# A four-layer graph network on one core: moved feature loads, wider-spaced row tiles, dense rows in two steps, and one last store

## The chip, the cores and the metric

The kernel runs on one core of one Trainium2 chip. The metric is the device time of one execution in microseconds (us). Beside it stands a profile of one execution: a page, and a trace that can be asked for waits, stretches and single instructions. The engines are called PE (matrix multiplication), DVE (VectorE), ACT (ScalarE), POOL (GpSimd) and SP (SyncE). DVE, ACT and POOL compute; SP only issues transfers here, and ACT and POOL issue some too.

## The reference

There are 2708 nodes with 512 features each, and one sparse matrix `adj`, stored densely. Four layers follow each other, each as `x = layernorm(x + layer(x))`, all in float32:

- Layer 0: `adj` plus its mask, scaled by row, times `x`, over the row's sum.
- Layer 1: attention and graph convolution, joined by two gates: `sigmoid(gate_a * (attn @ (x @ W_sa)) + gate_b * (adj @ (x @ W_gcn) + b))`, where the attention weights come from `exp(-leaky_relu(s_left + s_right))` on the entries of `adj` that are not zero.
- Layer 2: `x @ W0 + A x @ W1 + A A x @ W2 + A A A x @ W3`, so three products with `adj` in a row.
- Layer 3: `relu((D (adj + I) D @ x + x) @ W + b)`, with `D` from the degrees.

So nearly all of the work is seven products of a 2708 x 2708 matrix with a 2708 x 512 one.

## The kernel before, in words

**Tiling.** Rows of `adj` are cut into two halves of 1354, features into two halves of 256, so that every product is a 2 x 2 block product. It is done with seven block products instead of eight (the scheme of Strassen and Winograd): DVE first makes sums of the blocks of the moving matrix (`s1` to `s4`) and of the features (`T1` to `T4` from `B11`, `B12`, `B21`, `B22`, functions `x_sums` and `x_last`), PE then runs the seven products P1 to P7 into the PSUM banks `accu`, `accc`, `accd` and `acca`, and DVE adds the products to the result. Of the 1354 rows, ten tiles have 128 rows; the 74 rows that remain of each half are handled apart ("R" groups, loaded by `rest_x`, bank `accr`).

**Stages.** The seven products are stages S[0] to S[6]. Stages 0 to 2 are run by `sweep` over the four column ranges `RANGES` (0, 384, 768 and 1024, the last one 330 wide), stages 3 to 6 by `sweep2` over two column ranges `RANGES2` of 338 and 339 with more of the recursion. In the trace stage 0 begins at about 20 us, stage 1 at 429, stage 2 at 830, stage 3 at 1440, and stages 4, 5 and 6 at 1803, 2164 and 2525.

**Order.** `at(position, fn)` puts a piece of work on a list with a position; a stage is 28 positions long, and the list is sorted by position. Each piece then issues its instructions on the engines that it names, and a scheduler fixes the order of each engine from this list; for the first pieces of the kernel and for those marked `hold` (the last argument of `at`) the order of the list is binding. A position thus moves an instruction in its engine's queue, and sets no time. A load is queued on the engine that issues it, and if the load has to wait, everything behind it on that engine waits as well.

**What the change touches.**

- `next_x` (L252) loads the features of the next `sweep` stage. Row tiles 0 to 7 are loaded early; tiles 8 and 9 (group D) and the remainder rows come last, since their source rows were just written. All go on GpSimd's queue, through `x_load` and `rest_x`. The row tile itself (o, X) is normalised by `layernorm` (L552 to L566), whose power (L559) is a GpSimd instruction too, and written to X by GpSimd (`store`, L151).
- `next_x2` (L302) does the same for the `sweep2` stages; `rest` (in it) loads the remainder rows.
- `move` (L147) cuts a transfer in two, so that the first has a multiple of 16 rows:

```
c = m - m % 16 if m > 16 else m
queue.dma_start(out=dst[:c], in_=src[:c])
if c < m:
    queue.dma_start(out=dst[c:m], in_=src[c:m])
```

- `done1` (L994) finishes a column range of stage 1. For the first three ranges it takes pairs of row tiles (one of each half, 3, 3 and 2 of them), and makes the dense product of a pair by `seven` (L637), in two parts, each with matmuls (L644) and sums on DVE (L651). Around them stands the work of the next column range: its products (L457), sums of blocks (`comb`, L402), copies (L511) and sums (`add`, L518) of the products, and the degree tally `deg` (L963), which reads each adjacency tile as it arrives.
- `ext_sums` (L1169) makes four sums (L1180) of dense rows for the later stages: it loads four tiles of X2T (L1176, SP's queue) into tiles of a ring of 38, adds, and stores the sums as Es (L1181, GpSimd's queue). Around it stand the block sums of `sweep2` (z, L1218; t, L1252), the sums of the products (q, L1295; with `accr`, L1353), and the transposes and stores of Y (L1397, L1402).
- `done6` finishes stage 6: a dense product (`ps_d`, L605), two DVE operations (L1479, L1480), the normalisation with its last step on ACT (L564), and the store to `out`. The last row tile has 83 rows.

Of the kernel before, what the change touches and what calls it, by code (L numbers as in the profile page):

```python
# [27 lines left out]
NH = 1354  # L28
# [13 lines left out]
RANGES2 = [(0, 338), (676, 339)]  # L42
# [26 lines left out]
def gnn_kernel(ctx: ExitStack, tc: tile.TileContext, x, adjT, w_sa, a_sa, w_gcn, b_gcn, wab, bab, w_hop, w_out,  # L69
# [108 lines left out]
    def at(pos, fn, hold=False):  # L178

        def go():  # L180
            n = len(nc.cur_bb.bb.instructions)
            fn()
            held.update(range(n, len(nc.cur_bb.bb.instructions)))

        events.append((pos, len(events), go if hold else fn))
# [60 lines left out]
    def x_load(src, k, s, eng):  # L246
        w = wt(k)
        q = x_source(src, k)[("B11", "B12", "B21", "B22").index(s)]
        t = b12_tile(k) if s == "B12" else new_x(s, k)
        move(eng, t[:w], q)  # L250

    def next_x(base, src, sums=0.95, halves=-0.25):  # L252


        q = nc.gpsimd
        at(base + 1.3, lambda: rest_x(src, q))
        for k in range(KW):
            f = k / KT
            if (k * P) < RANGES[-1][0]:
                at(base - 5.8 + f, lambda k=k: x_load(src, k, "B11", q))  # L260
                at(base - 1.85 + f, lambda k=k: x_load(src, k, "B22", q))
                at(base - 1.84 + f, lambda k=k: x_load(src, k, "B12", q))
                at(base - 1.15 + f, lambda k=k: x_sums(k), True)
                at(base - 0.85 + f, lambda k=k: x_load(src, k, "B21", q))
                at(base + 1.5 + f, lambda k=k: x_last(k), True)
            else:
                at(base + halves + 0.05 * (k - 8), lambda k=k: x_load(src, k, "B22", q))
                at(base + max(halves, 0.1) + 0.05 * (k - 8), lambda k=k: x_load(src, k, "B21", q))
                at(base + sums + 0.03 * (k - 8), lambda k=k: x_sums(k), True)
                at(base + 2.6 + 0.03 * (k - 8), lambda k=k: x_last(k), True)  # L270

# [30 lines left out]
    def next_x2(base, src, ext_src=None, one=False, plus=False, swapped=False):  # L302

        q = nc.gpsimd
        m = RANGES2[1][0] // P
        early = {"B11": (-5.8, m), "B12": (-4.8, m)}
        if one:
            early["B22"] = (-0.95, RANGES[-1][0] // P)

        def go(s, ks, ext):  # L310
            for k in ks:
                x_load(src, k, s, q)
            if ext and ext_src is not None:
                c0 = HD if s in ("B12", "B22") else 0
                for i, g in enumerate("BD"):
                    r0 = (HD if s in ("B21", "B22") else 0) + i * P
                    h = "T3" if s == "B12" else s
                    if g == "D" and ks[-1] < 8:
                        group(h, g)
                    t, w = groups[h, g][0][:, 2, :], ext_src[r0 : r0 + P, :]  # L320
                    if not swapped:
                        nc.scalar.dma_start(out=t, in_=w[:, c0 : c0 + HD])
                        continue
                    for f in range(2):
                        nc.scalar.dma_start(out=t[:, f * P : (f + 1) * P].rearrange("p (c d) -> p c d", d=32),
                                            in_=w.rearrange("p (c f d) -> p f c d", c=4, d=32)[:, c0 // P + f, :, :])

        def residual(s):

            for i, g in enumerate("BD"):  # L330
                t = groups[s, g][0][:, 2, i * P : (i + 1) * P]
                nc.vector.tensor_tensor(t, t, ident, ALU.add)

        if plus:
            at(base - 1.4, lambda: residual("B22"), True)
            at(base + 1.9, lambda: residual("B11"), True)
        for s, p in (("B22", 0.0 if one else -1.95), ("B21", 0.02), ("B11", 1.6), ("B12", 1.8)):
            ks = list(range(KW))
            if s in early:
                lo, m = early[s]  # L340
                at(base + lo, lambda s=s, m=m: go(s, range(m), True))
                ks = range(m, KW)
            at(base + p, lambda s=s, ks=ks: go(s, ks, ks[0] == 0))

        def sums(g):
            i = slice(0, 2 if g in "BD" and ext_src is None else 3)
            part = lambda t: t[:, i, :]
            for s in ("T1", "T2", "T4"):
                group(s, g)
            t = {s: part(groups[s, g][0]) for s in SETS}  # L350
            nc.vector.tensor_tensor(t["T1"], t["T3"], t["B11"], ALU.subtract)
            nc.vector.tensor_tensor(t["T2"], t["B22"], t["T1"], ALU.subtract)
            nc.vector.tensor_tensor(t["T3"], t["B22"], t["T3"], ALU.subtract)
            nc.vector.tensor_tensor(t["T4"], t["B21"], t["T2"], ALU.subtract)
            for s in ("T1", "T2", "T3", "T4"):
                groups[s, g][1].update(range(3))

        def rest():
            for e in range(2):
                cols = slice(e * HD, (e + 1) * HD)  # L360
                for s in REST_HOMES[e]:
                    group(s, "R")
                t, t32 = (groups[s, "R"][0] for s in REST_HOMES[e])
                lo, hi = src[KT - 1], src[2 * KT - 1]
                rows_over(q, t, (lo[:, cols], hi[:, cols]))
                q.dma_start(out=t32, in_=copies(hi[KA - KR :, cols], 4))

        at(base + 1.75, rest)
        for i, g in enumerate("ACBD"):
            at(base + 4.2 + 0.3 * i, lambda g=g: sums(g), True)  # L370

# [566 lines left out]
    i = 0  # L938
# [55 lines left out]
    def done1(p0, dp, last, R0, n, h, C, tiles):  # L994
# [39 lines left out]
        for i, (t, lo, w) in enumerate(tiles):  # L1034
            H, y = {}, []

            def b7(part, t=t, lo=lo, w=w, H=H, y=y):
                if part == 0:
                    y.extend(nat("y") for _ in range(2))
                seven(part, Y, W[8], H, lo, w, y, None, [vec[1], vec[1]])  # L1040
                if part == 1:
                    for j in range(2):
                        finish(t + KT * (1 - j), w, y[j])

            at(p0 + 0.6 + 0.56 * i, lambda f=b7: f(0))
            at(p0 + 0.6 + 0.56 * i + 0.26, lambda f=b7: f(1))

    sweep(S[1], RANGES, extra=extra1, done=done1, late=0.85, save=True)

# [116 lines left out]
            move(nc.gpsimd, o[b : b + m, :], src[t][a : a + m, :])  # L1166
        return o

    def ext_sums(g, s, q):  # L1169

        n = RANGES2[g][1]
        E = {}
        for ij in ("11", "21", "22", "12"):
            E[ij] = ring_tile("a" + ij)
            e = (int(ij[1]) - 1) * HD + q * P
            nc.sync.dma_start(out=E[ij][:, :n], in_=X2T[g, int(ij[0]) - 1][e : e + P, s * n : (s + 1) * n])  # L1176
        E["s3"] = ring_tile("s3")
        for m, o, a, b, op in (("s3", "s3", "11", "21", ALU.subtract), ("s1", "21", "21", "22", ALU.add),
                               ("s2", "11", "21", "11", ALU.subtract), ("s4", "12", "12", "11", ALU.subtract)):
            nc.vector.tensor_tensor(E[o][:, :n], E[a][:, :n], E[b][:, :n], op)  # L1180
            nc.gpsimd.dma_start(out=SE[m, g, s][q * P : (q + 1) * P, :], in_=E[o][:, :n])  # L1181

# [197 lines left out]


    for i in range(4):
        at(S[2] + 19.5 + 1.1 * i, lambda i=i: ext_sums(0, i // 2, i % 2))
        at(S[3] + 7.0 + 1.3 * i, lambda i=i: ext_sums(1, i // 2, i % 2))

    def hop_done(dst):

# [77 lines left out]
    def done6(p0, dp, g, i0, n, h, cc, tiles):  # L1465

        end = (g, h) == (1, 0)
        for i, (s, lo, w) in enumerate(tiles[3:] + tiles[:3] if end else tiles):
            got = {}
            r0 = i0 + s * n + lo  # L1470

            def a(r0=r0, w=w, got=got):
                got["x"] = fetch2(X3, h, r0, w)

            def b(s=s, lo=lo, w=w, r0=r0, got=got):
                px = dense(lambda c: cc(s, c)[:, lo : lo + w], W[6], w)
                y = got["x"]
                r = 12 * g + 6 * h + 3 * s + lo // P
                nc.vector.scalar_tensor_tensor(px[:w], px[:w], rdeg_f[:w, r : r + 1], vec[6][:w], ALU.mult, ALU.add)  # L1479
                nc.vector.scalar_tensor_tensor(y[:w], px[:w], 0.0, y[:w], ALU.max, ALU.add)  # L1480
                layernorm([(y, 0, D)], y, w, True)
                move(nc.sync, out[h * NH + r0 : h * NH + r0 + w, :], y[:w])

            p = p0 - 0.095 + 0.14 * i if end else p0 + 0.1 + 0.28 * i
            at(p - 0.6, a)
            at(p, b)
# [57 lines left out]
```

## Time and profile before

| | |
|---|---|
| Median of 7 runs | 2900.22 us (2897.40 to 2902.28) |
| The profiled execution's own time | 2898.14 us |
| Its span, first to last instruction | 2896.3 us |
| Mean granted clock of PE | 0.996 |
| Busy, PE | 2843.6 us |
| Busy, DVE | 2242.1 us |
| Busy, POOL | 626.6 us |
| Busy, ACT | 564.9 us |

Times in the trace are counted from the first instruction. A line of the list of waits reads: engine, tile and line that waited, "<-", the engine (or transfer), tile and line that it waited for, then us in total, how often, and the longest. In a line of a timeline stand the start, the duration, the engine, the line, the operation with what it writes and reads, and in brackets how long the engine had stood idle and what ended that. A PE that is busy may still run at half its clock; the stretches list the granted clock beside the busy time.

### The profile page before, as it was taken

Reading aid. Unit: us, or ns where it says so; the run is one execution under the profiler, and the core shown is the slowest. Engines: PE = TensorE matmul, PEld = TensorE weight load, DVE = VectorE, ACT = ScalarE, POOL = GpSimd, SP = SyncE. Lnnn points to the kernel's source line nnn. Section 1 sums busy time; section 2 is a strip of 40 time slices with the busy share of each in tenths; the row PEclk is TensorE's granted clock in tenths of the full one; section 3 lists DMA queues with packets and bytes.
Section 4 is the critical chain, followed back from the end, with each engine's and each line's share of the span. In section 5 each row is a group of like instructions: output and inputs, shape, how many; then the busy total and the mean of one; then the engine's idle time right before and its main releaser. Section 6 shows DMA issues by size and latency. Waiting matters only on the chain. (4 is left out here: it accounts for less than half of the span.)

```text
span 2896.3 us, 37361 instructions
## 1 busy us (share of the span) xinstructions
PE 2843.6 (98%) x10847; PEld 1852.1 (64%) x10847; DVE 2242.1 (77%) x5780; ACT 564.9 (20%) x1106; POOL 626.6 (22%) x1133
## 2 busy tenths in 40 slices
PE   7999999999999999999999999999999999999998
PEld 6655665658765656766666666666666666665664
DVE  6989698667648675875689788887888878798776
ACT  4544200101137454651100000000000100100001
POOL 0223224123310101123113033030330212501102
PEclk9999999999999999999999999999999999999999
DMA  7666466355544333564667667566675665854551
GB/s 232 202 199 188 137 212 218 110 166 168 179 128 131 116 115 100 176 192 151 207 208 222 205 197 234 168 207 203 200 235 164 197 187 171 240 170 142 174 154 59
DMA packets 373145, 511.50 MB, mean 177 GB/s; under 512 B 64022, under 2 KB 326096, under 8 KB 372940
## 3 DMA queue, kind: packets, MB, share of 16 engines
q1 hardware_dynamic: 307128, 372.01, 43.5%
q0 software_dynamic: 50272, 127.29, 12.9%
q10 hardware_dynamic: 15540, 9.82, 1.2%
q8 instruction: 86, 1.41, 0.2%
q14 instruction: 119, 0.97, 0.1%
HBM read 425.22 MB, written 83.67 MB: 176 GB/s over the span
## 5 line engine op out<-in xcount | busy, mean ns | idle before, releaser
L1218 DVE TENSOR_TENSOR z<-z 128x339 f32<-128x339 f32 (+1 forms) x966 | 456.9, 506 | 12.0 <-PE accu L1271 3.3
L1289 ACT COPY q<-accu 128x338 f32<-128x338 f32 (+1 forms) x84 | 34.5, 443 | 1025.4 <-PE accu L1271 1025.4
L559 POOL TENSOR_TENSOR rstd<-rstd,neg_half 128x1 f32<-128x1 f32 (+3 forms) x92 | 59.2, 643 | 719.1 <-DVE rstd L558 713.4
L1271 PE MATMUL accc<-s,t 128*128 128x338 f32 (+1 forms) x644 | 198.3, 452 | 0.0
L1271 PE MATMUL accu<-z,t 128*128 128x338 f32 (+1 forms) x644 | 194.4, 448 | 0.6 <-DVE z L1218 0.6
L1271 PE MATMUL accc<-z,t 128*128 128x338 f32 (+1 forms) x644 | 193.7, 448 | 0.0
L1271 PE MATMUL accd<-z,t 128*128 128x338 f32 (+1 forms) x644 | 193.7, 448 | 0.0
L1402 POOL DMA_DIRECT2D Y<-y x192 | 104.8, 552 | 378.2 <-DVE y L1397 343.2
L402 DVE TENSOR_TENSOR a<-a,a 128x384 f32<-128x384 f32 (+2 forms) x330 | 162.9, 515 | 10.3 <-PE accu L457 8.9
L1271 PEld LDWEIGHTS accc<-s,t 128*128 128x128 f32 x644 | 121.5, 191 | 65.8 <-issue 8.9
L1271 PEld LDWEIGHTS accd<-z,t 128*128 128x128 f32 x644 | 122.3, 190 | 61.4 <-issue 1.8
L1271 PEld LDWEIGHTS accc<-z,t 128*128 128x128 f32 x644 | 122.1, 190 | 61.6 <-issue 2.4
L1271 PEld LDWEIGHTS accu<-z,t 128*128 128x128 f32 x644 | 121.7, 190 | 61.8 <-issue 1.9
L1218 DVE TENSOR_TENSOR s<-z 128x338 f32<-128x338 f32 (+1 forms) x322 | 150.3, 505 | 8.4 <-PE accc L1271 7.6
L1295 DVE TENSOR_TENSOR q<-q,accd 128x338 f32<-128x338 f32 (+1 forms) x112 | 56.4, 504 | 128.0 <-PE accd L1271 128.0
L1072 ACT ACTIVATE e<-row,neg_s 128x384 f32<-128x384 f32 (+5 forms) x176 | 100.4, 570 | 79.6 <-DVE e L1074 27.5
L1074 DVE TENSOR_TENSOR e<-e,f 128x384 f32<-128x384 f32 (+5 forms) x176 | 87.9, 509 | 22.6 <-ACT f L1073 21.5
L1073 ACT ACTIVATE f<-row,neg_s 128x384 f32<-128x384 f32 (+5 forms) x176 | 100.0, 568 | 27.0 <-PE accc L457 7.1
L963 DVE SCALAR_TENSOR_TENSOR deg<-a,deg 128x384 f32<-128x384 f32 (+2 forms) x152 | 75.2, 506 | 14.5 <-DMA a<-in_adjT 13.5
L605 PE MATMUL ps_d<-w,q 128*128 128x512 f32 (+2 forms) x192 | 85.7, 593 | 0.0
L1075 DVE SCALAR_TENSOR_TENSOR a<-a,e 128x384 f32<-128x384 f32 (+2 forms) x160 | 80.5, 510 | 3.5 <-DMA a<-in_adjT 1.2
L405 POOL DMA_DIRECT2D As<-a x120 | 64.9, 544 | 78.2 <-DVE a L402 68.4
(650 smaller groups left out, 5898.9 us busy)
## 6 DMA issues: line engine op xcount, KB each, us to landing
z<-As SPq DMA_DIRECT2D x320, 169.5 KB
z<-As SPq DMA_DIRECT2D x320, 169.0 KB
a<-in_adjT SPq DMA_DIRECT2D x240, 192.0 KB
z<-in_adjT SPq DMA_DIRECT2D x240, 169.5 KB
z<-in_adjT SPq DMA_DIRECT2D x240, 169.0 KB
a<-in_adjT SPq DMA_DIRECT2D x120, 165.0 KB
a<-in_adjT SPq DMA_DIRECT2D x112, 128.0 KB
As<-a POOLq DMA_DIRECT2D x60, 192.0 KB, 4.0
```

The lines of the kernel that those rows point to most:

```text
L402: nc.vector.tensor_tensor(A[r, dst, k][:, :n], A[r, a, k][:, :n], A[r, b, k][:, :n], op)
L405: nc.gpsimd.dma_start(out=SD[m][k * P : (k + 1) * P, R0 : R0 + n], in_=A[r, dst, k][:, :n])
L559: nc.gpsimd.tensor_tensor(rstd[:w, 1:2], rstd[:w, 0:1], neg_half[:w], ALU.pow)
L605: nc.tensor.matmul(o, lhs(c), r, start=c == 0 and n == 0, stop=c == DC - 1, skip_group_check=True)
L963: nc.vector.scalar_tensor_tensor(d[:w, :n], a[:w, :n], 0.0, d[:w, :n], ALU.not_equal, ALU.add)
L1072: nc.scalar.activation(e[:w, :n], row[R0, h][0][:w, :n], AF.Exp, bias=neg_s[:w, t : t + 1])
L1073: nc.scalar.activation(f[:w, :n], row[R0, h][1][:w, :n], AF.Exp, bias=neg_s01[:w, t : t + 1])
L1074: nc.vector.tensor_tensor(e[:w, :n], e[:w, :n], f[:w, :n], ALU.min)
L1075: nc.vector.scalar_tensor_tensor(a[:w, :n], a[:w, :n], 0.0, e[:w, :n], ALU.not_equal, ALU.mult)
L1218: nc.vector.tensor_tensor(d[:, :n], Z[x + (k,)][:, :n], Z[y + (k,)][:, :n], op)
L1271: nc.tensor.matmul(B[home][:, :n], stat(v, k), a[:, :n], start=bool(start and k == 0), stop=k == nk - 1, skip_group_check=True)
L1402: nc.gpsimd.dma_start(out=rows[:, :, f * P : (f + 1) * P], in_=o[32 * f : 32 * (f + 1), : m * P].rearrange("p (b d) -> p b d", d=P))
```

## The change

Five edits. Edit 1: at stage 1 alone, `next_x` issues the loads of group D (B22 and B21 of tiles 8 and 9) and those of the remainder rows on ACT's queue instead of GpSimd's. Edit 2: in `next_x2` the positions of the last loads of B11, B12 and of the remainder rows become 1.6, 1.75 and 1.75 (from 1.6, 1.8 and 1.75), and for stage 6 2.3, 2.45 and 2.45. Edit 3: in `done1` the pairs stand 1.1 positions apart instead of 0.56, and the second part of a pair 0.2 behind the first instead of 0.26. Edit 4: `ext_sums` is cut into `ext_loads` and `ext_sums`; in stage 2 the loads come 0.2 positions earlier than both did before and the sums 0.3 later, in stage 3 the loads 0.4 earlier and the sums 0.7 later. Edit 5: the last row tile of the last stage is stored by one transfer of 83 rows on ACT's queue, instead of `move` on SP's, which makes two of 80 and 3 rows.

```diff
@@ next_x
-        at(base + 1.3, lambda: rest_x(src, q))
+        ql = nc.scalar if base == S[1] else q
+        at(base + 1.3, lambda: rest_x(src, ql))
...
-                at(base + halves + 0.05 * (k - 8), lambda k=k: x_load(src, k, "B22", q))
-                at(base + max(halves, 0.1) + 0.05 * (k - 8), lambda k=k: x_load(src, k, "B21", q))
+                at(base + halves + 0.05 * (k - 8), lambda k=k: x_load(src, k, "B22", ql))
+                at(base + max(halves, 0.1) + 0.05 * (k - 8), lambda k=k: x_load(src, k, "B21", ql))
@@ next_x2
+        late = 2.3 if base == S[6] else 1.6
...
-        for s, p in (("B22", 0.0 if one else -1.95), ("B21", 0.02), ("B11", 1.6), ("B12", 1.8)):
+        for s, p in (("B22", 0.0 if one else -1.95), ("B21", 0.02), ("B11", late), ("B12", late + 0.15)):
...
-        at(base + 1.75, rest)
+        at(base + late + 0.15, rest)
@@ done1
-            at(p0 + 0.6 + 0.56 * i, lambda f=b7: f(0))
-            at(p0 + 0.6 + 0.56 * i + 0.26, lambda f=b7: f(1))
+            at(p0 + 0.6 + 1.1 * i, lambda f=b7: f(0))
+            at(p0 + 0.6 + 1.1 * i + 0.2, lambda f=b7: f(1))
@@ ext_sums
-    def ext_sums(g, s, q):
+    def ext_loads(E, g, s, q):
         n = RANGES2[g][1]
-        E = {}
         for ij in ("11", "21", "22", "12"):
...
             nc.sync.dma_start(out=E[ij][:, :n], in_=X2T[g, int(ij[0]) - 1][e : e + P, s * n : (s + 1) * n])
         E["s3"] = ring_tile("s3")
+    def ext_sums(E, g, s, q):
+        n = RANGES2[g][1]
         for m, o, a, b, op in (("s3", "s3", "11", "21", ALU.subtract), ("s1", "21", "21", "22", ALU.add),
...
     for i in range(4):
-        at(S[2] + 19.5 + 1.1 * i, lambda i=i: ext_sums(0, i // 2, i % 2))
-        at(S[3] + 7.0 + 1.3 * i, lambda i=i: ext_sums(1, i // 2, i % 2))
+        for g, p in enumerate((S[2] + 19.3 + 1.1 * i, S[3] + 6.6 + 1.3 * i)):
+            a = ({}, g, i // 2, i % 2)
+            at(p, lambda a=a: ext_loads(*a))
+            at(p + 0.5 + 0.6 * g, lambda a=a: ext_sums(*a))
@@ done6
-                move(nc.sync, out[h * NH + r0 : h * NH + r0 + w, :], y[:w])
+                o = out[h * NH + r0 : h * NH + r0 + w, :]
+                if end and i == 5:
+                    nc.scalar.dma_start(out=o, in_=y[:w])
+                else:
+                    move(nc.sync, o, y[:w])
```

More of the change, by code (lines that the diff above doesn't have):

```diff
@@ L1473, in a, with b @@
                 got["x"] = fetch2(X3, h, r0, w)
-            def b(s=s, lo=lo, w=w, r0=r0, got=got):
+            def b(i=i, s=s, lo=lo, w=w, r0=r0, got=got):
                 px = dense(lambda c: cc(s, c)[:, lo : lo + w], W[6], w)
```

## The prediction

> **What bounds the kernel now.** I read the page first, then the waits of the whole span for PE, then the waits and the timeline around each PE stall that a changed line touches, then the stretches with their granted clock, last the tail.
>
> ```profile
> span 2896.3 us, 37361 instructions
> ...
> PE 2843.6 (98%) x10847; PEld 1852.1 (64%) x10847; DVE 2242.1 (77%) x5780; ACT 564.9 (20%) x1106; POOL 626.6 (22%) x1133
> ```
>
> PE is busy for 98% of the span, and no edit changes its work. What can be won or lost is therefore only the start, the time in which PE stands still, the stretches in which its clock is halved, and the tail. The waits of PE that touch changed lines:
>
> ```profile
> PE ps_n L588 <- DVE P1c L518: 4.1, 1, 4.1
> ...
> PE accr L1342 <- DVE q L1353: 2.5, 1, 2.5
> PE ps_n L1378 <- DVE q L1295: 1.8, 1, 1.8
> ...
> PE ps L644 <- DVE y L651: 1.4, 3, 0.7
> ```
>
> The longer waits of the list (on masks, on r) lie in stage 0, which no edit reaches. Four waits remain: 4.1 us between stages 0 and 1, 2.5 us in stage 3, 1.8 us before stage 6, 1.4 us at the pairs of stage 1. The stretches show what follows a stall (columns: length, then busy time of PE, PEld, DVE, ACT and POOL, granted clock, DMA share, GB/s):
>
> ```profile
> 431.70:436.70 5.00, 0.82 (x6) 0.61 (x6) 5.00 (x14) 0.00 (x0) 2.67 (x6) 1.00 0.60 227
> 436.70:440.20 3.50, 3.50 (x10) 2.17 (x9) 3.50 (x8) 0.00 (x0) 3.50 (x7) 0.51 0.71 217
> ...
> 1523.00:1525.60 2.60, 0.29 (x2) 0.00 (x0) 2.60 (x8) 0.00 (x0) 2.60 (x6) 1.00 0.89 255
> 1525.60:1532.40 6.80, 6.60 (x17) 3.39 (x18) 6.80 (x19) 0.00 (x0) 5.04 (x10) 0.50 0.66 202
> 2525.00:2529.10 4.10, 2.23 (x8) 0.96 (x7) 3.43 (x10) 0.00 (x0) 2.06 (x5) 1.00 0.67 206
> ```
>
> After each long stall the clock stands at 0.50 for 3.4 us, in stage 3 for 6.8 us. A half-clock stretch of 3.4 us does 1.7 us of work, so it costs 1.7 us on top of the stall, twice that in stage 3. The smallest stall with such an end is the last row: 4.10 - 2.23 = 1.9 us idle. The Trainium skill, page "TensorE: Matmul & The Clock Gate", section "What's actually happening", says that the clock falls after at least one idle window of about 3.4 us; the 2.5 us stall of stage 3 and the 1.9 us one contradict that here. By that rule neither would have had a half-clock stretch, and the clock terms below would be nothing.
>
> **Edit 1, loads on ACT's queue at stage 1.** The 14 transfers that the edit moves leave GpSimd's list (1138 to 1124 instructions) and stand on ACT's, ten of them before the copies of L891. The order on PE and DVE is unchanged up to there. Waits around it, then GpSimd's timeline:
>
> ```profile
> POOL B22D L151 <- DMA X<-o: 4.5, 1, 4.5
> PE ps_n L588 <- DVE P1c L518: 4.1, 1, 4.1
> DVE o L566 <- POOL rstd L559: 2.6, 1, 2.6
> ```
> ```profile
> 421.31 0.54 POOL L405 DMA_DIRECT2D As<-s  x1 [0.22 <-issue]
> 426.37 0.54 POOL L151 DMA_DIRECT2D B22D<-X  x1 [4.52 <-DMA X<-o]
> ...
> 427.99 0.56 POOL L559 TENSOR_TENSOR rstd<-rstd,neg_half 74x1 f32<-74x1 f32 x1
> ```
>
> GpSimd stands 4.5 us at the B22D load, because that load must wait until its row tile has landed. Queued behind it are two B21A loads and the small power L559, whose operand DVE finished at 425.69. DVE waits for L559 until 428.59 and then runs without a gap to the sum P1c L518 at 435.27, for which PE waits. Without the B22D load, L559 can start at about 425.8 and DVE at 426.4: 2.2 us earlier. PE's 4.1 us become 1.9, no longer in one stretch before the clock is judged, so I also take off the 1.7 us: -3.9. Bounds: -2.2 (half-clock stretch stays) and -5.8 (the whole stall goes). What is late next is DVE itself, busy for all 5.00 us of the stretch. ACT now waits for the landing, and the P1c copies L511 queue behind it; they ran at 450.8, the last landing was at 454.5, and they are first read some 40 us later, so I put this at nothing; without that cover it is up to 454.5 - 450.8 = +3.7.
>
> **Edit 2, later loads of the next stages.** In the order of the queues only the loads of the remainder rows change places with neighbours of their own kind. Needed long after: 0, with an end of +0.6 for one load issue in front of another.
>
> **Edit 3, pairs of row tiles.** In the first three column ranges of stage 1 the second and third pair move later between the products, and a pair's parts come closer: four matmuls instead of six between them for the third. The 1.4 us of waits on L651 are the most that can go. Against it, these sums now come behind the tallies L963, which over stage 1 wait 13.5 us in 13 waits for adjacency loads, 2.3 us at longest. Between -1.4 and one such wait, +2.3; I take -0.8, as the three waits for L651 are 0.7 at most each, and the tallies in the same stretch (575 to 720 us) wait only 2.3 us, 1.0 at most.
>
> **Edit 4, loads and sums of dense rows apart.** In stage 3, DVE's timeline:
>
> ```profile
> 1513.66 0.51 DVE L1180 TENSOR_TENSOR s<-a,a 128x339 f32<-128x339 f32 x1 [3.31 <-DMA a<-X2T]
> ...
> 1525.24 1.75 DVE L1353 TENSOR_TENSOR q<-q,accr 128x338 f32<-128x338 f32 x4
> ```
>
> DVE waits 3.31 us for a transfer issued less than 5 us before, then works off a queue without a gap until L1353, which PE's accr needs. In the new order the four sums (4 x 0.42 = 1.7 us) stand behind L1353 and the loads are issued earlier: L1353 could come 5.0 us sooner, and PE waits for 2.5. Both half-clock stretches go with it: -(2.5 + 6.8/2) = -5.9. Bounds: -2.0 (four sums moved, but the load's wait falls elsewhere in the same queue) and -6.2. The same split in stage 2 covers waits that stop no PE. Costs: SP issues four X2T loads ahead of z loads (0.4 us each, in a stage whose SP runs far ahead), GpSimd's Es stores come after Y stores, five of the ring's tiles are held about 15 us longer. I put them at 0; if the ring ran out it would be a z wait like that of stage 6, +1.9.
>
> **Edit 5, the last store.** Here one transfer of 83 rows on ACT's queue replaces two on SP's.
>
> ```profile
> 2890.36 0.33 SPq L151 DMA_DIRECT2D out<-ld  x1
> 2890.81 0.27 SPq L153 DMA_DIRECT2D out<-ld  x1
> ```
> ```profile
> DMA packets 144, 0.26 MB, mean 77 GB/s; under 512 B 16, under 2 KB 16, under 8 KB 144
> ```
> ```profile
> DMA packets 102, 0.17 MB, mean 90 GB/s; under 512 B 19, under 2 KB 19, under 8 KB 102
> ```
>
> The second answer is the 128-row store just before, the third these two transfers. The small packets end each engine's share: 16 for 128 rows, and 19 = 16 + 3 for 80 and 3 rows. So the shares were equal: 8, 5 and 1 rows. 83 is prime, and equal shares exist only on one engine. The 128-row store moved its 8 rows per engine in 0.79 us with packets of 0.08 us: 83 x 0.08 = 6.6 us in place of the 0.78 that the two transfers took, less 0.45 for the second issue: +5.4, and with a little slack between packets +5.9. Bounds: -0.4, if 83 rows spread as 80 do, and 83 x 0.15 - 1.2 = +11.2 at the packet spacing of the 80 rows (0.78 us for 5). I take +5.9, since all three rows show equal shares. The Trainium skill, page "DMA: Bandwidth & Descriptors", section "Why a DMA increments its semaphore by 16 and not by 1", gives as the number of engines the largest up to 16 that divides the row count; it speaks against this edit, by it 83 rows use one engine, and the sum would keep the positive term.
>
> **Sum.** -3.9 + 0 - 0.8 - 5.9 + 5.9 = -4.7. The profiled execution took 2898.14 (span 2896.33 and 1.8 around it), so 2893.4; the median of seven runs is 2.1 above it, so 2895.5. What a measurement can tell from no change is about 0.2%, 5.8 us: faster means under 2894.4, slower over 2906.0.
>
> **Rivals.** (a) The last store spreads over 16 engines: -11.0, 2889.2. For it: no row shows 83 rows. Against: the equal shares. Chance 0.3. (b) The removed waits only move: DVE was busy through both stalls, so another late operand takes half of each, -4.9, with the slow store +1.0: 2901.2. For it: DVE 77% busy and full in both stretches. Against: it stood idle 2.6 and 3.3 us ahead of them. Chance 0.2. (c) Slower: the sums L651 of the pairs queue behind tallies that wait for adjT, in each of the three ranges; PE stops for 2.3 us and loses 1.7 us by the clock each time, +12.0. With the rest (-3.9 - 5.9 + 5.9) +8.1: 2908.3. It decides once the pairs stop PE for more than 9.7 us in all; the 1.4 us now speak against it. Chance 0.12. (The forecast: 0.38.)
>
> **How the numbers follow.** Faster: a third of the forecast's spread (its bounds reach 2 us either way for edits 1 and 3, more for the store), nearly all of (a): 0.43. Slower: most of (c) and a little of (b) with the store at its upper end: 0.10. The rest, 0.47, is within 0.2%. The range 2886 to 2904 takes in (a) with 3 us below it and (b) with 3 above; outside lie (c) and the far ends.
>
> **What would show it.** Right: no POOL wait at B22D, L559 at about 426, PE's wait for P1c under 2 us and the clock at full speed from 436.7 to 440.2; no PE wait for L1353 and no half-clock stretch at 1525; the last store's data over 6 to 7 us and under half a dozen small packets in it. Wrong: a new wait of PE at ps L644 or at accu L457 in stage 1; a z wait in stage 3; data of the last store within 1 us, which alone would take the time to 2889; a packet time of 0.15 us there, which would take it to 2901.

## The result and the profile after

The changed kernel takes 2908.35 us (median of 14 runs, 2905.58 to 2912.51) against 2899.18 us for the kernel before (34 runs of the same comparison): 1.0033 times as long, 95% interval 1.0026 to 1.0040, so +9.6 us (7.5 to 11.6). The forecast was 2895.5, and the range ended at 2904.

The page after, first line and busy times:

```profile
span 2906.9 us, 37389 instructions
...
PE 2844.0 (98%) x10847; PEld 1850.6 (64%) x10847; DVE 2240.8 (77%) x5780; ACT 563.7 (19%) x1106; POOL 618.9 (21%) x1119
```

PE's work is the same (2844.0 us busy against 2843.6), and the span is 10.6 us longer. Line numbers shift by a few from kernel to kernel: L654 here is L651 before, L647 is L644. The waits of PE after, those that touch the change:

```profile
PE ps L647 <- DVE y L654: 8.1, 4, 3.2
PE pv L891 <- DVE ld L818: 4.4, 1, 4.4
...
PE ps_n L591 <- DVE P1c L521: 1.9, 1, 1.9
PE ps_n L1383 <- DVE q L1300: 1.8, 1, 1.8
```

The stall at P1c fell from 4.1 to 1.9 us and the one at accr (2.5 us) is gone, as forecast. Two are new or larger: 4.4 us at pv, and 8.1 us at the pairs, against 1.4. The stretches after (columns as before):

```profile
431.70:436.70 5.00, 2.99 (x15) 2.01 (x15) 3.77 (x9) 0.00 (x0) 2.69 (x5) 1.00 0.79 237
439.20:445.80 6.60, 2.19 (x18) 1.88 (x17) 2.40 (x5) 1.75 (x6) 0.54 (x1) 1.00 0.61 208
445.80:449.20 3.40, 3.40 (x6) 1.71 (x6) 3.25 (x10) 0.65 (x2) 0.90 (x2) 0.50 0.16 63
...
1520.00:1527.00 7.00, 7.00 (x26) 4.65 (x25) 5.86 (x17) 0.00 (x0) 4.37 (x8) 1.00 0.75 210
```

The half-clock stretch after P1c did not go: it now follows the stall at pv, 9 us later. Stage 3 runs at full clock.

Where the 10.6 us come from is read by comparing the start of the same PE instruction (by its number) in the two traces, each of one execution:

| Stretch (us of before) | Change |
|---|---|
| 405 to 525, start of stage 1 | +2.5 |
| 525 to 847, pairs of stage 1 | +6.7 |
| 1248 to 1329, end of stage 2 | +2.5 |
| 1449 to 1569, stage 3 | -5.6 |
| 2251 to 2292, between stages 5 and 6 (a 1.2 us wait of PE on ACT that some kernels show and some do not) | -1.4 |
| 2452 to 2573, around stage 6 | +2.0 |
| From the start of the last ACT operation (L564 before, L567 after) to the end: 6.81 and 10.69 | +3.9 |

### The profile page after: what moved, and what is told of

The parts are those of the page before. It is cut to its first block, busy times and chain, and to the rows that moved or that the text cites. A ratio compares the mean times of both kernels' runs of the same rounds, so it can differ in the third digit from the quotient of the medians.

```text
span 2906.9 us, 37389 instructions
## 1 busy us (share of the span) xinstructions
PE 2844.0 (98%) x10847; PEld 1850.6 (64%) x10847; DVE 2240.8 (77%) x5780; ACT 563.7 (19%) x1106; POOL 618.9 (21%) x1119
```

## The experiments

All are compared with runs of the kernel before on the same chip; the difference in us is the ratio times the median of those runs, with its 95% interval. Its median differed between chips, from 2899 to 2903.5 us. Each kernel has a short name, e1 to e13.

### Each edit by itself

**Edit 1 alone (e1_load_queue):**

```diff
+        ql = nc.scalar if base == S[1] else q
+        at(base + 1.3, lambda: rest_x(src, ql))
...
+                at(base + halves + 0.05 * (k - 8), lambda k=k: x_load(src, k, "B22", ql))
+                at(base + max(halves, 0.1) + 0.05 * (k - 8), lambda k=k: x_load(src, k, "B21", ql))
```

> Edit 1 alone on the kernel before. Theory (SP is held up): the moved loads wait on ACT for their source rows, and SP's later transfers wait for them to land, although they share no data; so SP's loads of the next adjacency tiles come about 8 us late, DVE's tally L963 waits about 8 us for one of them, PE stops about 4 us at pv, and the stall at P1c shrinks from 4.1 to 1.9 us as forecast. Time +2 to +3 us on the kernel before. Rival (the forecast): only the stall shrinks, nothing new: -3.9 us. If the late adjacency loads in the changed kernel came from the other edits, SP does not wait for ACT's loads here.

Measured: -0.3 us (-2.9 to +2.3): no gain, and not the +2 to +3 us of the theory. The trace shows the waits that the theory names: P1c waits 2.1 us, pv 3.9 us and the half clock follows it, 2.3 us lost from 405 to 525 us; the end of this kernel is 2.4 us shorter, which the theory left out (below, the end of the kernel). The same waits stand in the changed kernel, where SP's queue and DVE show them best. First SP's waits at 418 to 448 us, then a line of the waits at 415 to 460 us:

```profile
SPq L153 <- DMA B22D<-X: 6.2, 1, 6.2
SPq L396 <- DMA B21R<-X: 3.9, 1, 3.9
SPq L396 <- DMA r<-in_adjT: 3.9, 1, 3.9
SPq L299 <- DMA B11R<-X: 3.1, 1, 3.1
```
```profile
DVE deg L966 <- DMA a<-in_adjT: 7.9, 1, 7.9
```

SP waits for loads that ACT issued, into tiles that SP's own loads do not touch. The program that is built from the kernel says why. The transfers of SP and ACT take eight completion semaphores (DMAHW0 to 7) in turn, and each transfer first waits until the one before it on the same semaphore has landed. GpSimd's take another set (DMASW). From the list of the changed kernel:

```
ACT  B22D<-X (128x256)                waits DMAHW1, DMASW6
SP   r<-in_adjT (10x384), L153        waits DMAHW1
ACT  B11R<-X (32x256)                 waits DMAHW7, DMASW3, PE
SP   r<-in_adjT (128x1x384), L299     waits DMAHW7, PE
```

The B22D load was issued at 426.02, when its source had landed, and landed itself at 428.06; SP's L153, next in its queue from 421.88, started at 428.08. The loads of the next adjacency tiles thus came late, by 7.9 us (SP in the kernel before, then in the changed kernel):

```profile
425.09 4.41 SPq L393 DMA_DIRECT2D a<-in_adjT  x5
```
```profile
432.96 9.96 SPq L396 DMA_DIRECT2D a<-in_adjT  x5
```

DVE stood 7.9 us at a tally, and the sum ld L818 behind it kept PE.

**Edit 3 alone (e2_pairs):**

```diff
+            at(p0 + 0.6 + 1.1 * i, lambda f=b7: f(0))
+            at(p0 + 0.6 + 1.1 * i + 0.2, lambda f=b7: f(1))
```

> Edit 3 alone. Theory (the pairs starve): the second part of a pair's matmuls waits for DVE's sums of the first part, which stand behind block sums and tallies; PE waits for L651 at the second and third pairs by 1.4 to 3.2 us each, about 8 us in all against 1.4, some 0.9 us less at pg: +6 to +7 us. Rival (edit 1's late loads shift the adjacency loads and make these stalls): then edit 3 alone costs under 2 us. Forecast: -0.8 us.

Measured: +4.4 us (+1.7 to +6.7). PE waits for L651 by 1.4, 1.8, 1.5 and 3.0 us, and behind the last of them its clock stood at 0.50 for 3.4 us, from 793 us on. So the stalls belong to this edit, not to edit 1.

**Edit 4 alone (e3_ext_split):**

```diff
+        for g, (p, d) in enumerate(((S[2] + 19.3 + 1.1 * i, 0.5), (S[3] + 6.6 + 1.3 * i, 1.1))):
+            a = ({}, g, i // 2, i % 2)
+            at(p, lambda a=a: ext_loads(*a))
+            at(p + d, lambda a=a: ext_sums(*a))
```

> Edit 4 alone. Theory: in stage 3 the stall of 2.5 us at accr and both half-clock stretches go, -5.6 us; in stage 2 the X2T loads stand ahead of the adjacency loads and the sums come in another order, which costs about 2.4 us near 1290 to 1330 us (PE waits for block sums L402 and for the running sum L756); -3 us in all. Rival: the 2.4 us near 1300 come from other edits; then -5.6 us.

Measured: -5.2 us (-7.5 to -2.6). Stage 3 is as forecast, and the wait near 1290 us is there too. A stretch of stage 3, then PE's wait at 1285 to 1325 us:

```profile
1520.00:1530.00 10.00, 10.00 (x44) 5.96 (x44) 9.28 (x26) 0.44 (x1) 8.70 (x16) 1.00 0.75 210
```
```profile
PE accd L457 <- DVE a L402: 1.5, 3, 0.7
```

By the same PE instructions, this trace loses 2.4 us between 1205 and 1305 us. The kernels that leave the order of stage 2 alone lose nothing there. In stage 3 it gains 5.4 us on the one trace of the kernel before; in the nine other traces without this edit the same stretch (1449 to 1569) took 0.0 to 2.5 us longer than there, so that trace was a quick one. This fits a measured gain that is larger than the -3 of the theory.

**Edit 5 alone (e4_last_store):**

```diff
+                if end and i == 5:
+                    nc.scalar.dma_start(out=o, in_=y[:w])
```

> Edit 5 alone. Theory: the store runs on one engine and lands 6.7 us later, but before, GpSimd's closing drain ended 3.2 us after the last landing and set the end, so only the rest shows: +3.9 us. Rival (the forecast): the whole of it shows, +5.9 us. The work of the kernel up to the store takes as long as before.

Measured: +4.6 us (+2.0 to +7.3). In the trace 10.59 us lie between the start of the last ACT operation and the end, against 6.81 in the kernel before: +3.8.

**Edit 2 alone (e5_late_loads):**

```diff
+        late = 2.3 if base == S[6] else 1.6
...
+        at(base + late + 0.15, rest)
```

> Edit 2 alone. The forecast put it at nothing: a few remainder loads change places on GpSimd's queue. Theory: within 0.1% (3 us) of the kernel before. Rival: the stalls of PE near 2487 and 2550 us in the changed kernel (z, 1.0 and 2.3 us) come from it: about +2 us, with these stalls in the trace.

Measured: +1.5 us (-1.2 to +4.1), unclear, and no new stall near 2550 us (0.6 us there). The 1.0 and 2.3 us waits near 2487 and 2550 us are found in kernels without this edit too, e6_gpsimd_later (below) for one.

### The queue of the late loads

The edit in place of edit 1 (e6_gpsimd_later):

```diff
-                at(base + halves + 0.05 * (k - 8), lambda k=k: x_load(src, k, "B22", q))
+                at(base + halves + 0.05 * (k - 8), lambda k=k: x_load(src, k, "B22", q), base == S[1])
...
-    next_x(S[1], X1)
+    next_x(S[1], X1, halves=0.0)
```

> In place of edit 1, the two B22 loads of group D stay on GpSimd's queue at stage 1 and are listed later (position 0.0 instead of -0.25, order binding), behind the small power L559. Theory (SP was held up by the completion semaphores that it shares with ACT): the forecast's mechanism holds once ACT is left out of it: L559 about 2.2 us earlier, PE's stall at P1c from 4.1 to about 1.9 us, SP waits for none of these loads, no stall at pv, -2 to -4 us on the kernel before. Rival (whatever is done there, DVE's queue gives the time back a few us later, for instance through the tally L963): a new stall of about 4 us as in the changed kernel, no gain.

Measured: -1.7 us (-4.6 to +0.9); the time alone leaves it open. The trace does not: L559 starts at 425.33, PE's wait at P1c is 1.9 us, there is none at pv, SP waits for none of these loads, and no half-clock stretch follows. From GpSimd's timeline, the waits and the stretches:

```profile
425.33 0.61 POOL L559 TENSOR_TENSOR rstd<-rstd,neg_half 74x1 f32<-74x1 f32 x1 [2.91 <-DVE rstd L558]
```
```profile
PE ps_n L588 <- DVE P1c L518: 1.9, 1, 1.9
```
```profile
436.70:440.20 3.50, 3.50 (x24) 2.70 (x23) 2.79 (x7) 0.80 (x4) 3.50 (x7) 1.00 0.76 274
```

Both kernels free L559 from the blocked load; only where ACT issued the loads did SP come late. By the same PE instructions, the stretch from 405 to 525 us is 3.4 us shorter than before here, and 3.1 and 2.0 us shorter in two later kernels with the same loads, e8_best and e12_fewer_gpsimd. The difference between those two is the clock: a stall of 2.1 us at P1c brought a half-clock stretch of 3.4 us in e12 and none in e8.

### The pairs taken out, and taken apart

The changed kernel without edit 3 (e7_without_pairs):

```diff
-            at(p0 + 0.6 + 1.1 * i, lambda f=b7: f(0))
-            at(p0 + 0.6 + 1.1 * i + 0.2, lambda f=b7: f(1))
+            at(p0 + 0.6 + 0.56 * i, lambda f=b7: f(0))
+            at(p0 + 0.6 + 0.56 * i + 0.26, lambda f=b7: f(1))
```

> The changed kernel with edit 3 undone. Theory (the edits add up, as far as each is known from its own run: edit 1 -0.3, edit 4 -5.2, edit 5 +4.6, and 2.4 us more at the end, since edit 1's shorter closing drain of GpSimd is hidden behind the long store): about +1.5 us on the kernel before, so 7 to 8 us under the changed kernel. Rival (the pairs cost little by themselves, and the late adjacency loads of edit 1 cost most): +5 us or more, with stalls of PE at L651 in the old layout too.

Measured: +1.2 us (-1.5 to +3.8) on the kernel before, as the sum of the single edits said. Without edit 3, the changed kernel is a draw. By this run edit 3 costs 8.4 us in the changed kernel (9.6 less 1.2), against 4.4 alone; the intervals overlap, and whether it costs more beside the other edits stays open.

Edit 3 has two halves. The distance alone (e9_wide_pairs):

```diff
-            at(p0 + 0.6 + 0.56 * i, lambda f=b7: f(0))
-            at(p0 + 0.6 + 0.56 * i + 0.26, lambda f=b7: f(1))
+            at(p0 + 0.6 + 1.1 * i, lambda f=b7: f(0))
+            at(p0 + 0.6 + 1.1 * i + 0.26, lambda f=b7: f(1))
```

> Half of edit 3: the pairs 1.1 apart, the second part still 0.26 behind the first. Theory (what hurts is how few matmuls lie between the parts at the later pairs and that the third pair comes into the next product, while DVE works off block sums and tallies): with 1.1 and 0.26 the parts lie about as close as with 0.2 on PE (two column steps apart), so most of edit 3's +4.4 us stays: +2 to +5 us, waits of PE for L651 of 4 us or more. Rival (the parts' closeness, 0.2, is the whole cost): within 2 us of the kernel before.

Measured: +6.4 us (+3.5 to +9.0). The closeness alone (e10_near_parts):

```diff
-            at(p0 + 0.6 + 0.56 * i + 0.26, lambda f=b7: f(1))
+            at(p0 + 0.6 + 0.56 * i + 0.2, lambda f=b7: f(1))
```

> The other half of edit 3: the pairs 0.56 apart as before, the second part 0.2 behind the first. Theory as for e9_wide_pairs: small, 0 to +2 us. Rival (closeness is the whole cost): +4 us, with waits of PE for L651 of 4 us or more.

Measured: +0.9 us (-1.7 to +3.5). So the distance costs; what closeness costs is not clear of noise. PE's waits at 570 to 800 us, e9_wide_pairs first, then e10_near_parts:

```profile
PE ps L644 <- DVE y L651: 6.5, 4, 2.0
```
```profile
PE ps L644 <- DVE y L651: 3.5, 2, 2.1
```

I took it that too little product work covered the sums between the parts, and gave the pairs of e9_wide_pairs more of it (e13_wide_far_parts, the lines against e9_wide_pairs):

```diff
-            at(p0 + 0.6 + 1.1 * i + 0.26, lambda f=b7: f(1))
+            at(p0 + 0.6 + 1.1 * i + 0.6, lambda f=b7: f(1))
```

> The pairs 1.1 apart as in edit 3, the second part 0.6 behind the first in place of 0.2, so that eight more matmuls of the products lie between the two parts. Theory (PE starves because the second part needs banks that DVE has not yet read: the first part's sums come late among block sums and tallies, and too little product work covers them): with that cover PE's waits for L651 fall under 2 us, and the time is within 2 us of the kernel before, 4 to 6 us under e9_wide_pairs. Rival (the place of the pairs as such costs: wherever the parts lie, DVE's later work and the loads behind it are shifted): the waits only move to other lines, +4 us or more as in e9_wide_pairs.

Measured: 1.0051 (1.0037 to 1.0065), +14.8 us (+10.7 to +18.9). My theory falls, and the rival came. The waits at L644 are gone altogether, and stand elsewhere (PE's waits at 429 to 830 us):

```profile
PE ds L977 <- DVE y L651: 6.5, 2, 4.6
PE ps_r L921 <- DVE y L651: 5.3, 2, 4.3
```

The same DVE sums, L651, now keep the tiles ds and ps_r, which come from the same ring of eight PSUM banks, for longer than they kept the second part. In the same trace the clock stood at 0.50 for 10.2 us from 593.5 us on, 3.4 us from 713 and 6.8 us from 812. PE was busy for 16.7 us of these, so some 8 us of work were lost there beside the waits.

The sums come late wherever the second and third pair are moved further into the product; there DVE works off block sums and tallies. The tallies themselves wait longer for adjacency loads there. DVE's waits from 575 to 720 us, in the kernel before and in the changed kernel:

```profile
DVE deg L963 <- DMA a<-in_adjT: 2.3, 3, 1.0
```
```profile
DVE deg L966 <- DMA a<-in_adjT: 10.7, 5, 5.2
```

The same sum is 9.9 to 10.2 us in the other three kernels with pairs 1.1 apart (e2, e9, e13), and 2.3 to 5.2 us in all kernels with pairs 0.56 apart. Shortly ahead of three of the changed kernel's four stalls DVE had waited at such a tally (0.6, 3.6 and 1.5 us); ahead of the fourth, of 1.4 us at 695.71, it had only worked for some 4 us. The last range (DVE, then PE):

```profile
794.47 0.50 DVE L966 SCALAR_TENSOR_TENSOR deg<-a,deg 128x330 f32<-128x330 f32 x1 [1.47 <-DMA a<-in_adjT]
794.89 0.42 DVE L654 TENSOR_TENSOR y<-ps,y 128x256 f32<-128x256 f32 x1
```
```profile
795.36 1.13 PE L647 MATMUL ps<-w,W 128*128 128x256 f32 x4 [3.16 <-DVE y L654]
```

The sum that PE waits for stands behind a tally that waits 1.47 us for its tile. That range has two pairs, and before, the last of their matmuls had begun by 784 us.

### The end of the kernel

The last store on ACT's queue, but in two transfers (e11_split_on_act, the lines against e4_last_store):

```diff
-                    nc.scalar.dma_start(out=o, in_=y[:w])
+                    move(nc.scalar, o, y[:w])
```

> The last store on ACT's queue, but cut into 80 and 3 rows as before. Theory (the end is set by GpSimd's closing drain, 6.87 us from its last power on, and the store had landed 3.2 us ahead of that): from the start of ACT's last operation to the end 6.8 us, as before, to 0.1 us. Rival (the landing of the store sets the end, as the forecast had it): up to 0.4 us less. Both say: the 3.8 us of edit 5 come from the 83 rows in one transfer, not from ACT's queue.

Measured, in one execution: 6.82 us from the start of ACT's last operation to the end, 2898.56 us in all. The 83 rows in one transfer are the cost, not ACT's queue. The transfer in the changed kernel:

```profile
DMA packets 84, 0.17 MB, mean 19 GB/s; under 512 B 1, under 2 KB 1, under 8 KB 84
```

One small packet ends it where the two transfers before had 19: one engine moved all 83 rows, at 27 GB/s while it ran (13 packets of 2 KB in a microsecond). This agrees with the rule that the prediction named, from the Trainium skill, page "DMA: Bandwidth & Descriptors", section "Why a DMA increments its semaphore by 16 and not by 1": the number of engines is the largest up to 16 that divides the row count, so one for 83 rows.

What follows the last power on GpSimd is its closing drain, a DRAIN instruction near the end of its program. Its longest in the kernel before, the changed kernel, e1_load_queue and e12_fewer_gpsimd (the third number, in ns):

```profile
L1540 POOLq DRAIN  x3: 46/102/6872, 2888.7 to 2896.1; - x3
```
```profile
L1551 POOLq DRAIN  x3: 46/106/4503, 2895.4 to 2906.6; - x3
```
```profile
L1541 POOLq DRAIN  x3: 46/102/4503, 2894.5 to 2899.5; - x3
```
```profile
L1544 POOLq DRAIN  x3: 46/102/4995, 2884.9 to 2890.4; - x3
```

Before, the last store had landed at 2892.37 and the drain ended at 2895.55: 3.2 us of the store's new length are hidden. In the twelve kernels whose last store is split, the span ends 0.8 us after this drain; in the three that store 83 rows at once (the changed kernel, e4, e7), it ends 1.0 to 1.1 us after the landing. With edit 1 the drain is 2.4 us shorter, but the changed kernel cannot use it, since its store lands at 2905.79.

### A kernel that beats both

The loads of e6_gpsimd_later with edit 4 in stage 3 alone (e8_best); the lines of the second part:

```diff
-        at(S[2] + 19.5 + 1.1 * i, lambda i=i: ext_sums(0, i // 2, i % 2))
-        at(S[3] + 7.0 + 1.3 * i, lambda i=i: ext_sums(1, i // 2, i % 2))
+        for g, (p, d) in enumerate(((S[2] + 19.5 + 1.1 * i, 0.0), (S[3] + 6.6 + 1.3 * i, 1.1))):
+            a = ({}, g, i // 2, i % 2)
+            at(p, lambda a=a: ext_loads(*a))
+            at(p + d, lambda a=a: ext_sums(*a))
```

> The loads of e6_gpsimd_later, and edit 4 in stage 3 alone; no other edit. Theory: the gain of e6_gpsimd_later (-2 to -4 us) and the stage 3 part of edit 4 (-5.5 us) add up: -8 to -9 us, no half-clock stretch at 1525 us and no stall near 1290 us. Rival (gain given back further on): -5 us or less.

Measured: 2893.92 us, -8.1 us (-11.3 to -4.6). And with the 12 small copies on ACT (e12_fewer_gpsimd, the lines against e8_best):

```diff
-                nc.gpsimd.dma_start(out=t[a:b, o : o + 1], in_=t[r : r + b - a, c : c + 1])
+                nc.scalar.dma_start(out=t[a:b, o : o + 1], in_=t[r : r + b - a, c : c + 1])
```

> e8_best, and the 12 small copies of L935 are issued by ACT instead of GpSimd, 1023 transfers on GpSimd's queue in place of 1035. Theory (the closing drain is shorter when GpSimd has issued fewer transfers: 4.50 us in the three kernels with 1021, 6.87 in the seven with 1035): the drain takes 4.5 to 5 us and the time is 1.9 to 2.4 us under e8_best. Rival (the drain's length goes with the kind of the moved loads, or ACT's copies at 718 to 732 us come late): 6.87 us, no gain.

Measured: 2888.11 us, 0.9959 (0.9946 to 0.9971), -11.9 us (-15.7 to -8.4). From the start of the last ACT operation to the end it is 4.93 us, against 6.80 in e8_best: the 1.9 us that the drain is shorter. The two medians come from two chips; what more they differ by is within the intervals.

## Why the prediction was wrong

- **What bounds it: right.** PE's work stayed; every difference is a stall, a half-clock stretch or the tail.
- **Edit 1, -3.9: wrong.** L559 came at 425.84 (forecast 425.8) and P1c's stall became 1.9, as forecast. The step that failed is the cover: "ACT now waits for the landing ... so I put this at nothing". It asked what queues behind the waiting loads on ACT, and not what waits for their completion semaphores on SP. The 4.4 us stall at pv and, behind it, a half-clock stretch that costs 1.7 us came in its place: +2.5 instead of -3.9 at this boundary. With ACT left out, e6's trace gains 3.4 us there, so the rest of the chain was sound. On ACT itself the delay was larger than the +3.7 named as the most, the P1c copies ran at 460.96 instead of 450.81, but no wait of PE came of it. That no half-clock stretch followed the shorter stall was luck: the prediction's own rows have one behind 1.9 us of idle, and in e12 one followed 2.1 us at this very place.
- **Edit 3, -0.8: wrong, and of the wrong sign.** +4.4 alone, +6.7 in the changed kernel's trace. The step that failed is the price of the new place: I took it from the waits of the old order, "the tallies in the same stretch (575 to 720 us) wait only 2.3 us, 1.0 at most". With the pairs moved they waited 10.7 us, 5.2 at most, and PE waited 8.1 us for L651, 3.2 at most. What DVE works off ahead of the sums, and the banks that the pairs hold meanwhile, were left out too; how much is due to the late loads and how much to DVE's own work, no run separates. Rival (c) named the place and the instructions, and the sign of being wrong, a new wait at ps L644, came. That its total, 2908.3, meets the measured 2908.35 is luck: its 12 us for the pairs were too much (in the changed kernel's trace no stall at the pairs lowered the clock; in e2 and e9 one did), and its -3.9 for edit 1 was wrong the other way.
- **Edit 4, -5.9: right in stage 3** (-5.6 in the trace), wrong in stage 2. There it was said to cover "waits that stop no PE" at no cost; the new order made PE wait for block sums, +1.8 to +2.4 in the three traces that have it (1205 to 1305 us).
- **Edit 5, +5.9: mechanism right, end wrong.** One engine, 83 packets of 2 KB, all but the first few 0.08 us apart; with the pauses among the first dozen the data took 7.6 us, not 6 to 7. The landing came 9.59 us after ACT's last operation began, against 2.85: +6.7, more than the +5.9 of the term. But the term counted the later landing in full. Before, 4.0 us lay between the landing and the end, and most of that was a drain that runs beside the store: +3.8 alone.
- **Edit 2, nothing:** within what a comparison can tell.
- **The sum.** The single edits add up to -0.3 + 1.5 + 4.4 - 5.2 + 4.6 = +5.0; the 2.4 us of drain that edit 1 gains alone and loses beside the long store make it +7.4, a tenth under the measured 7.5 to 11.6, with each term known to some 2.5 us only. Of the trace's 10.6 us, edit 1 as forecast would have left about +4, edit 3 as forecast about +3, both within 0.2%; the two together, about -3.
- **Open:** why stage 6 and the time around 2487 to 2550 us differ by 1 to 2 us from kernel to kernel, with the same instructions; why the tallies wait longer for their loads once the pairs are moved; and what edit 1 adds at the pairs (in the first column range of the old layout PE stalled by 3.5 us in e1 and 2.2 in e7, the two kernels with edit 1, and by 0.7 to 1.2 in the others).

## What to carry to other kernels

When a load that has to wait is moved to another engine's queue, ask not only what stands behind it there but what shares its completion semaphore: here ACT's queue held up SP's without a byte in common. Read the end of a kernel engine by engine: the last landing was not what set it, and a term for a later landing counts only beyond whatever else is still closing. Work put off until later in a stage lands in another engine's backlog. The waits read in the old order do not price the new place (2.3 us of tallies became 10.7 here): look at what that engine does there, and count the banks that stay taken meanwhile.

## What the hardware showed that I had not expected

- GpSimd's closing drain was longer, the more transfers GpSimd had issued in the whole program: 6.87 us with 1035 (eleven kernels), 4.99 with 1023 (one), 4.50 with 1021 (three): 0.16 us for each of the 12 small copies, 0.17 for each of the 14 loads of edit 1. Moving 12 tiny copies to another queue, 2 ms ahead of the end, shortened the end by 1.9 us. Three counts cannot tell whether it goes by the transfers or by something that comes with them, such as their rows.
- Stalls of PE of 1.3 to 2.3 us went either way with the clock. A half-clock stretch followed 1.3 us in e10 (at 1310), 1.9 us in the kernel before (at 2525.65) and 2.1 us in e12 (at P1c); none followed 2.1 us in e8 at P1c, nor, in e6, 1.9 us at 431.35, 1.9 at 2525.64 and 2.3 at 2544.02. The Trainium skill, page "TensorE: Matmul & The Clock Gate", section "What's actually happening", says that the window is free-running; that fits stalls of one length with both outcomes.
